# A Laplace neural operator layer and an involution block: VectorE's order in the forward transform written out by hand, its table work cut into 242 steps

## The chip, the cores and the metric

The kernel runs on one core of a Trainium2 chip. A core has five engines that run side by side, each through its own list of instructions in order: TensorE (PE, matmuls), VectorE (DVE), ScalarE (ACT), GpSimd (POOL) and SyncE (SP, which here issues DMAs; GpSimd issues some as well). They wait for one another through semaphores. Matmuls write to a small memory, PSUM; everything else lies in SBUF (128 partitions). The metric is device time in microseconds of the whole kernel, lower is better.

## What is computed

Two residual layers on x of 16 images, 16 channels, 256 x 256, float32. The first, which the change concerns, is a Laplace neural operator on the group-normalised input:

```python
alpha = jnp.fft.fft2(x, axes=(-2, -1))
A = 1.0 / (omega1[:, None, None, None] - weights_pole1[None])
Bm = 1.0 / (omega2[:, None, None, None] - weights_pole2[None])
S = jnp.einsum('ikpq,oikp,xikq->oxik', weights_residue, A, Bm)
output_residue1 = jnp.einsum('biox,oxik->bkox', alpha, S)
C = jnp.einsum('biox,oikp->bikpx', alpha, A)
D = jnp.einsum('bikpx,xikq->bikpq', C, Bm)
output_residue2 = jnp.einsum('bikpq,ikpq->bkpq', D, weights_residue)
x1 = jnp.fft.ifft2(output_residue1, s=(Ny, Nx), axes=(-2, -1)).real
E1 = jnp.exp(weights_pole1[..., None] * tyc)
E2 = jnp.exp(weights_pole2[..., None] * txc)
F = jnp.einsum('kbpq,bipz->kbiqz', output_residue2, E1)
x2 = jnp.einsum('kbiqz,biqx->kizx', F, E2).real
return x1 + x2 / Nx / Ny
```

The second layer (convolutions, mish, involution, a channel gate) is not touched.

## The kernel before

Four stages follow one another: `layer0_forward` (Fourier transform, about 0 to 1378 us of the profiled execution), `layer0_mix` (spectrum times the table of S, to about 2900), `layer0_back` (inverse transform, to about 3560) and `layer1`. The change lies in the first.

`layer0_forward` takes 64 steps, one for each image b and each group cg of four channels; two neighbouring channels make one normalisation group. A step does this:

- `fetch` (called for the input two steps ahead) loads z by SP and takes its BN statistics (L174) and aggregates (L176) on VectorE.
- `halves` (for the next step) normalises. `group_norm_scalars` sums over partitions with two small matmuls, gn_mean (L34) and gn_var (L42); VectorE works on each result (L36 to L39, then L44 and L47 to L53, with a square root on ScalarE at L46 between). Then VectorE adds the image's two halves, less the mean (L191), and GpSimd subtracts them (L194, 128 x 1024): both parts are the tile eo, which has two buffers.
- `rows`, twice for two channels each: for each channel 16 matmuls on pu (L207) and pv (L214), ScalarE copies half of pu to `right` (L222), and VectorE adds and subtracts it into u (L224, two instructions). pu has two buffers. ScalarE evicts pv as v, scaled (L231).
- `poles`: matmuls on v (L241), multiplied on VectorE (t, L252) and added up on GpSimd (acc, L265 to L267).
- `columns`: for the previous image's u, matmuls (L313), evictions on ScalarE (o, L320), stores by GpSimd (L329). Eight frequencies a step, nine in each fourth; the first four steps have none. The tile px has two buffers, which the tables' matmuls share.
- `finish`, once an image, closes the pole sums.

Beside the steps stand tables that depend on the weights alone. Two, `table("1")` and `table("2")`, are needed by `rows` and `poles` and made at the start (L135 to L140 on VectorE, matmuls L149, copies L158 and L160). Three more are needed by later stages and are written to DRAM in `tables`, a generator: residues (td, 16 channels, VectorE L415 to L426, matmuls L437), planes of A (avd, 33, L466 to L490) and exponentials (ed, 2 x 8 pairs of channels, L515 to L534, with `exponential` at L766 to L783). From step 4 on the main loop takes one piece of it in each step: 16 pieces with a residue each, 11 of three planes, 16 of a pair of exponentials, one kind after the other.

What sets the order: within `manual_schedule`, the engines named in it (here TensorE alone) run their instructions as the program is written. For the other engines a scheduler at build time orders them, and can put a table's instruction, or the statistics of an input, far from where it is written.

Of the kernel before, what the change touches and what calls it, by code (L numbers as in the profile page):

```python
# [72 lines left out]
def layer0_forward(ctx, tc, d, al, bd, tabs):  # L73
# [105 lines left out]
    def halves(b, cg, z, mv):  # L179

        if cg == 0:
            scales[b] = sm.tile([P, G], F32, tag="rs", name="rs")
        rs = scales[b][:, 2 * cg : 2 * cg + 2]
        nm = sm.tile([P, 2], F32, tag="nm", name="nm")
        yield from group_norm_scalars(nc, sm, psn, ones, mv, 2, nm, rs)
        nm2 = sm.tile([P, 2], F32, tag="nm2", name="nm2")
        nc.vector.tensor_scalar(nm2, nm, 2.0, None, ALU.mult)
        eo = ep.tile([P, 2, 4, N], F32, tag="eo", name="eo")
        for g in range(2):
            cs = slice(2 * g, 2 * g + 2)  # L190
            nc.vector.scalar_tensor_tensor(  # L191
                eo[:, 0, cs], z[:, cs, 0], nm2[:, g : g + 1], z[:, cs, 1], ALU.add, ALU.add
            )
        nc.gpsimd.tensor_tensor(eo[:, 1], z[:, :, 0], z[:, :, 1], ALU.subtract)  # L194
        yield eo, rs

    def rows(b, cg, j, eo, rs):
# [3 lines left out]
        for a in range(2):  # L201
# [21 lines left out]
            for h, sign in ((0, ALU.add), (1, ALU.subtract)):  # L223
# [5 lines left out]
                )  # L229
        vt = vp.tile([P, 2, 2, P], F32, tag="v", name="v")  # L230
# [105 lines left out]
    with tc.manual_schedule(engines={mybir.EngineType.PE}):  # L336
# [3 lines left out]
        *_, ready = halves(*steps[0], *fetched.pop(0))  # L340
        pieces = tables(ctx, tc, d, psx, tabs)
        acc = rsc = None
        for i, (b, cg) in enumerate(steps):
            now, following = ready, iter(())
            if i + 1 < len(steps):
                following = halves(*steps[i + 1], *fetched.pop(0))
                next(following)
            v0 = rows(b, cg, 0, *now)
            next(following, None)
            if b and cg == 0:  # L350
                rsc = finish(b - 1, acc)
            v1 = rows(b, cg, 1, *now)
            ready = next(following, None)
# [5 lines left out]
            poles(cg, (v0, v1), acc)  # L359
            if b:  # L360
# [4 lines left out]
            if i >= 4:  # L365
                next(pieces, None)
# [16 lines left out]
def tables(ctx, tc, d, psum, tabs):  # L383
# [5 lines left out]


    krow = load(nc, cp, d["krow_t"], [P, N], "krow_t")
    w = frequencies(nc, cp, d["tx"], krow, [P, N], "wt")
    sign = load(nc, cp, d["sign_t"], [P, 1], "sign_t")
    qr = cp.tile([P, C], F32, name="tqr")
    qi = cp.tile([P, C], F32, name="tqi")
    rr = cp.tile([P, C, M], F32, name="trr")
    ri = cp.tile([P, C, M], F32, name="tri")
    for t in range(2):
        ps = slice(64 * t, 64 * t + 64)
        nc.sync.dma_start(out=qr[ps], in_=d["p2r_iq"])  # L400
        nc.sync.dma_start(out=qi[ps], in_=d["p2i_iq"])
        nc.sync.dma_start(out=rr[ps], in_=d["rr_iq"])
        nc.sync.dma_start(out=ri[ps], in_=d["ri_iq"])
    nc.vector.tensor_scalar(qi, qi, sign, None, ALU.mult)
    nri = cp.tile([P, C, M], F32, name="tnri")
    nc.vector.tensor_scalar(nri, ri, sign, None, ALU.mult)
    nc.vector.tensor_scalar(ri, nri, -1.0, None, ALU.mult)
    q2 = cp.tile([P, C], F32, name="tq2")
    nc.vector.tensor_tensor(q2, qr, qr, ALU.mult)
    mt = load(nc, cp, d["mt"], [P, 2, 16], "mt")  # L410
    for k in range(C):
        e = tp.tile([P, N], F32, tag="te", name="te")
        r = tp.tile([P, N], F32, tag="trec", name="trec")
        br = tp.tile([P, N], F32, tag="tbr", name="tbr")
        nc.vector.tensor_scalar(e, w, qi[:, k : k + 1], None, ALU.add)  # L415
        nc.vector.tensor_tensor(r, e, e, ALU.mult)
        nc.vector.tensor_scalar(r, r, q2[:, k : k + 1], None, ALU.add)
        nc.vector.reciprocal(r, r)
        nc.vector.tensor_scalar(br, r, qr[:, k : k + 1], -1.0, ALU.mult, ALU.mult)
        nc.vector.scalar_tensor_tensor(e, e, -1.0, r, ALU.mult, ALU.mult)  # L420
        wts = []
        for h in range(2):
            wt = tp.tile([P, 2, 2, 16, M], F32, tag=f"wt{h}", name="wt")
            shape = [P, 16, M]
            for part, c, coef in ((0, 0, rr), (0, 1, ri), (1, 0, nri), (1, 1, rr)):
                nc.vector.tensor_tensor(  # L426
                    wt[:, part, c],
                    mt[:, h].unsqueeze(2).to_broadcast(shape),
                    coef[:, k].unsqueeze(1).to_broadcast(shape),
                    ALU.mult,  # L430
                )
            wts.append(wt)
        yield
        ps = psum.tile([P, 2, N], F32, tag="px", name="pt")
        for h, wt in enumerate(wts):
            for part, rhs in ((0, br), (1, e)):
                nc.tensor.matmul(  # L437
                    ps[:, h],
                    lhsT=wt[:, part].rearrange("p c i m -> p (c i m)"),
                    rhs=rhs,  # L440
                    start=part == 0,
                    stop=part == 1,
                )
        t = tp.tile([P, 2, N], F32, tag="tt", name="tt")
        nc.scalar.copy(t, ps)
        nc.sync.dma_start(out=td[:, :, k], in_=t)

    krow = load(nc, cp, d["krow_m"], [P, N], "krow_m")  # L450
    w = frequencies(nc, cp, d["ty"], krow, [P, N], "wm")
    sign = load(nc, cp, d["sign_m"], [P, 1], "sign_m")
    pr = cp.tile([P, 32], F32, name="tpr")
    pi = cp.tile([P, 32], F32, name="tpi")
    for q in range(4):
        nc.sync.dma_start(out=pr[32 * q : 32 * q + 32], in_=d["p1r_ip"])
        nc.sync.dma_start(out=pi[32 * q : 32 * q + 32], in_=d["p1i_ip"])
    nc.vector.tensor_scalar(pi, pi, sign, None, ALU.mult)
    pr2 = cp.tile([P, 32], F32, name="tpr2")
    nc.vector.tensor_tensor(pr2, pr, pr, ALU.mult)  # L460
    npr = cp.tile([P, 32], F32, name="tnpr")
    nc.vector.tensor_scalar(npr, pr, -1.0, None, ALU.mult)
    for g in range(NF):
        four = [P, 32, 4]
        e = tp.tile(four, F32, tag="ae", name="ae")
        nc.vector.tensor_tensor(  # L466
            e,
            w[:, 4 * g : 4 * g + 4].unsqueeze(1).to_broadcast(four),
            pi.unsqueeze(2).to_broadcast(four),
            ALU.add,  # L470
        )
        r = tp.tile(four, F32, tag="ar", name="ar")
        nc.vector.tensor_tensor(r, e, e, ALU.mult)
        nc.vector.tensor_tensor(r, r, pr2.unsqueeze(2).to_broadcast(four), ALU.add)
        nc.vector.reciprocal(r, r)
        av = tp.tile([P, 32, 4, 3], F32, tag="av", name="av")
        half = [64, 32, 4]
        nprb = npr.unsqueeze(2)
        nc.vector.tensor_tensor(av[:64, :, :, 1], r[:64], nprb[:64].to_broadcast(half), ALU.mult)
        nc.vector.tensor_tensor(av[64:, :, :, 1], r[64:], e[64:], ALU.mult)  # L480
        nc.vector.scalar_tensor_tensor(
            av[:64, :, :, 0].rearrange("p k f -> p (k f)"),
            e[:64].rearrange("p k f -> p (k f)"),
            -1.0,
            r[:64].rearrange("p k f -> p (k f)"),
            ALU.mult,
            ALU.mult,
        )
        nc.vector.tensor_tensor(av[64:, :, :, 0], r[64:], nprb[64:].to_broadcast(half), ALU.mult)
        nc.vector.tensor_scalar(av[:, :, :, 2], av[:, :, :, 0], -1.0, None, ALU.mult)  # L490
        nc.sync.dma_start(out=avd[g], in_=av.rearrange("p k f l -> p (k f l)"))
        if g % 3 == 2:
            yield


    phase = load(nc, cp, d["phase"], [P, 1], "phase")
    turn = cp.tile([P, 1], F32, name="turn")
    nc.vector.tensor_scalar(turn, phase, TWO_PI, None, ALU.mult)
    last = load(nc, cp, d["last"], [P, 1], "last")
    c1 = 6.28125  # L500
    c2 = float(np.float32(TWO_PI - c1))
    for i, axis in enumerate("12"):
        pr = cp.tile([P, C], F32, name=f"epr{axis}")
        pi = cp.tile([P, C], F32, name=f"epi{axis}")
        for a in range(2):
            nc.sync.dma_start(out=pr[64 * a : 64 * a + 64], in_=d[f"p{axis}r_kp"])
            nc.sync.dma_start(out=pi[64 * a : 64 * a + 64], in_=d[f"p{axis}i_kp"])
        tr = cp.tile([P, N], F32, name=f"etr{axis}")
        nc.sync.dma_start(out=tr, in_=d["ty" if axis == "1" else "tx"].to_broadcast([P, N]))
        for k in range(0, C, 2):  # L510
            arg = tp.tile([P, 2, N], F32, tag="arg", name="arg")
            n = tp.tile([P, 2, N], F32, tag="n", name="n")
            nf, af = n.rearrange("p k x -> p (k x)"), arg.rearrange("p k x -> p (k x)")
# [1024 lines left out]
```

## Time and profile before

| | |
|---|---|
| three runs | 7063.57, 7067.28, 7080.53 us (median 7067.28) |
| profiled execution | 7081.88 us in all, span 7080.1 us |
| mean TensorE clock | 0.976 of full |
| busy share: TensorE, VectorE, ScalarE, GpSimd | 92%, 79%, 54%, 50% |

The forward transform from 70 to 1380 us holds TensorE 1202.7 us busy, VectorE 1058.5, ScalarE 428.9, GpSimd 578.2.

How to read the views that follow: in the table of groups a row is a line of the kernel, an engine, an operation, the tiles written and read, its count, its busy time and its mean. In the timeline a row is start, duration, engine, line and operation; in brackets how long the engine stood idle before it and what ended that. Weight loads of TensorE have rows of their own. Times are microseconds from the start of the span, and of this one execution. Line numbers are those of the kernel before; in the changed kernel the lines below L182 are moved by two and more.

### The profile page before, as it was taken

What the parts mean: (1) busy time and instruction counts of PE and PEld (TensorE: products, weight loads), DVE (VectorE), ACT (ScalarE), POOL (GpSimd) and SP (SyncE); (2) the same over time, 40 slices, a digit from 0 to 9 for tenths busy, and PEclk for the clock granted to TensorE, in tenths of its full rate; (3) what the DMA queues carried; (4) which work ended last, traced back from release to release, by engine and by line L of the source; (5) the groups of instructions that cost most, each with busy time, mean ns of one, the idle gap of its engine ahead of it and who ended that gap; (6) DMA issues with size and microseconds to landing.
All of it is one profiled execution on the core that took longest, in us unless ns stands there. A gap on an engine that the chain in (4) does not pass through costs nothing. (4 is left out here: it accounts for less than half of the span.)

```text
span 7080.1 us, 144599 instructions
## 1 busy us (share of the span) xinstructions
PE 6544.7 (92%) x55592; PEld 3663.3 (52%) x55592; DVE 5608.9 (79%) x10346; ACT 3835.5 (54%) x5996; POOL 3521.3 (50%) x4614
## 2 busy tenths in 40 slices
PE   7889999899999998899979999999999999999996
PEld 5777778666667666677733333333333333333331
DVE  8999985466667666688878888888888888888885
ACT  2223333365666665322266666666666676666671
POOL 2334445412222222466655666667666667665663
PEclk9899999999999999999989999999999999999998
DMA  3344444433333333699968888889888889888886
GB/s 99 112 115 123 125 120 123 132 95 92 100 99 102 98 96 92 207 326 326 326 191 248 260 257 269 277 278 282 268 257 265 277 281 278 277 258 264 277 272 212
DMA packets 716083, 1443.41 MB, mean 204 GB/s; under 512 B 98954, under 2 KB 525254, under 8 KB 673638
## 3 DMA queue, kind: packets, MB, share of 16 engines
q1 hardware_dynamic: 567206, 959.76, 44.3%
q0 software_dynamic: 148192, 474.40, 21.3%
q8 instruction: 444, 7.27, 0.4%
q14 instruction: 241, 1.97, 0.1%
HBM read 877.12 MB, written 556.47 MB: 202 GB/s over the span
## 5 line engine op out<-in xcount | busy, mean ns | idle before, releaser
L1085 ACT ACTIVATE wide<-c,b 32x512 f32<-32x512 f32 x2176 | 1477.6, 679 | 314.0 <-PE c L1037 265.2
L1116 DVE TENSOR_TENSOR top<-pd,t 32x512 f32<-32x512 f32 x2176 | 1504.0, 691 | 55.8 <-DMA cf<-top 3.2
L1037 PE MATMUL c<-z,w 102*128 102x512 f32 x2048 | 996.4, 618 | 110.5 <-ACT wide L1085 89.0
L1113 DVE TENSOR_TENSOR t<-pd,r 64x512 f32<-64x512 f32 x1088 | 743.8, 684 | 349.0 <-PE pd L1105 322.8
L1097 POOL COPY wide<-wide 32x1031 f32<-32x1031 f32 (+1 forms) x576 | 581.2, 1009 | 882.6 <-ACT wide L1085 855.5
L1105 PE MATMUL pd<-wide,dw 128*128 128x512 f32 x2048 | 994.4, 607 | 13.0 <-DVE top L1116 12.0
L720 POOL DMA_DIRECT2D hd<-h x512 | 323.5, 639 | 1207.1 <-DVE h L713 1182.6
L1037 PEld LDWEIGHTS c<-z,w 102*128 102x128 f32 x2048 | 370.6, 191 | 695.2 <-issue 457.9
L1185 PE MATMUL c2ps<-rows,c 128*32 128x512 f32 x6144 | 721.9, 602 | 5.6 <-DVE odd L1212 5.6
L1105 PEld LDWEIGHTS pd<-wide,dw 128*128 128x128 f32 x2048 | 382.8, 193 | 576.5 <-issue 417.2
L1056 ACT ACTIVATE bot<-c,b 128x512 f32<-128x512 f32 x544 | 343.9, 683 | 462.2 <-issue 383.3
L1098 POOL COPY wide<-wide 32x1031 f32<-32x1031 f32 (+1 forms) x576 | 574.0, 997 | 33.5
L700 PE MATMUL ph<-ix,yt 64*128 64x256 f32 x4128 | 506.6, 393 | 6.1 <-issue 5.4
L643 PE MATMUL ps<-tt,lt 128*64 128x256 f32 x4224 | 495.4, 385 | 13.3 <-DMA tt<-td 10.4
L313 PE MATMUL px<-wxn,u 128*64 128x256 f32 x4224 | 482.9, 380 | 8.1 <-ACT o L320 8.1
L207 PE MATMUL pu<-fy,eo 128*128 128x128 f32 x2048 | 427.0, 292 | 26.4 <-DVE u L224 21.8
L700 PEld LDWEIGHTS ph<-ix,yt 64*128 64x128 f32 x4128 | 395.9, 191 | 93.7 <-issue 46.1
L1185 PEld LDWEIGHTS c2ps<-rows,c 128*32 128x32 f32 x6144 | 175.4, 109 | 513.3 <-issue 407.8
L873 POOL TENSOR_TENSOR x<-x,o 128x512 f32<-128x512 f32 x256 | 323.7, 1265 | 217.4 <-DVE o L872 199.3
L607 DVE TENSOR_SCALAR alb<-alc,m 128x1024 f32<-128x1024 f32 x330 | 420.0, 1397 | 0.0
L214 PE MATMUL pv<-at,eo 128*128 128x128 f32 x2048 | 413.9, 285 | 0.0
L651 DVE COPY s<-ps 128x512 f32<-128x512 f32 x264 | 265.4, 1023 | 186.9 <-PE ps L643 169.7
(220 smaller groups left out, 11732.0 us busy)
## 6 DMA issues: line engine op xcount, KB each, us to landing
rows<-cf SPq DMA_DIRECT2D x128, 2176.0 KB
z<-zn SPq DMA_DIRECT2D x768, 257.8 KB
cf<-top POOLq DMA_DIRECT2D x512, 240.0 KB, 6.8
cf<-bot POOLq DMA_DIRECT2D x96, 840.0 KB, 11.0
alc<-al SPq DMA_DIRECT2D x264, 256.0 KB
zn<-zb SPq DMA_DIRECT2D x128, 516.0 KB
o<-zn SPq DMA_DIRECT2D x128, 516.0 KB
z<-in_x SPq DMA_DIRECT2D x64, 1024.0 KB
```

What stands on the lines that cost most here:

```text
L207: nc.tensor.matmul(pu[:, xh, e].rearrange("p v m -> p (v m)"), lhsT=lhs, rhs=fy[:, e], start=True, stop=True,)
L313: nc.tensor.matmul(ps[64 * k : 64 * k + 64, :, h], lhsT=u[:, h, part, g0 + j + k].rearrange("p f c -> p (f c)"), rhs=wxn[:, h, part], star ...
L643: nc.tensor.matmul(ps[64 * h : 64 * h + 64, v], lhsT=lt[:, h, k, 1 - v : 3 - v].rearrange("p l f c -> p (l f c)"), rhs=tt[:, h, k], start= ...
L700: nc.tensor.matmul(ph[q][:, e], lhsT=yt[lanes, i].rearrange("p t k -> p (t k)"), rhs=ix[lanes, i], start=n == 0, stop=n == 3,)
L1037: nc.tensor.matmul(ps[:, a], lhsT=w, rhs=z[:k, c : c + 2, 0:N], start=True, stop=True)
L1085: nc.scalar.activation(self.feat[64 - 32 * q : 96 - 32 * q, f, self.groups[g], :H], ps[q][32 * f : 32 * f + 32], AF.Mish, bias=b1[0][32 * ...
L1097: nc.gpsimd.tensor_copy(flat[0:32, f, 1:m], flat[64:96, f, 0 : m - 1])
L1098: nc.gpsimd.tensor_copy(flat[96:128, f, 0 : m - 1], flat[32:64, f, 1:m])
L1105: nc.tensor.matmul(ps, lhsT=dwt if self.tail else dw, rhs=self.feat[:, f, cs, :H], start=True, stop=True,)
L1113: nc.vector.tensor_tensor(t[64:128], ps[:64], self.r[:, cs], ALU.mult)
L1116: nc.vector.tensor_tensor(self.top[32 * f : 32 * f + 32, cs, q], ps[lanes], t[lanes], ALU.add)
L1185: nc.tensor.matmul(ps[32 * j : 32 * j + 32], lhsT=w[:, blk], rhs=src[:, 4 * j + blk : 4 * j + blk + 4, x : x + H], start=(i, blk) == (0, 0 ...
```

## The change

VectorE joins TensorE in `manual_schedule`, so its instructions now run as written. What is written changes with it:

- The second half of `group_norm_scalars` (variance, root, scale) moves from between the two calls of `rows` to after `poles`; the sums and differences eo come directly after the mean.
- `tables` becomes three generators, residues, planes and exponentials, cut much finer and merged in equal proportion into 242 steps (64 places for residues, of which 49 have work, 66 for planes, 112 for exponentials). `rows` takes one behind each channel's u, from step 2 on: four a step, so that the last is taken in step 62.
- Scalings by a value per partition in the tables move from VectorE to ScalarE.

```diff
@@ halves
-        yield from group_norm_scalars(nc, sm, psn, ones, mv, 2, nm, rs)
+        scalars = group_norm_scalars(nc, sm, psn, ones, mv, 2, nm, rs)
+        next(scalars)
...
         yield eo, rs
+        yield from scalars
@@ rows
-    def rows(b, cg, j, eo, rs):
+    def rows(b, cg, j, eo, rs, between):
...
+            next(between, None)
         vt = vp.tile([P, 2, 2, P], F32, tag="v", name="v")
@@ main loop
-    with tc.manual_schedule(engines={mybir.EngineType.PE}):
+    with tc.manual_schedule(engines={mybir.EngineType.PE, mybir.EngineType.DVE}):
...
             if i + 1 < len(steps):
                 following = halves(*steps[i + 1], *fetched.pop(0))
-                next(following)
-            v0 = rows(b, cg, 0, *now)
-            next(following, None)
+                ready = next(following)
+            v0 = rows(b, cg, 0, *now, pieces if i >= 2 else iter(()))
             if b and cg == 0:
                 rsc = finish(b - 1, acc)
-            v1 = rows(b, cg, 1, *now)
-            ready = next(following, None)
+            v1 = rows(b, cg, 1, *now, pieces if i >= 2 else iter(()))
...
             poles(cg, (v0, v1), acc)
+            next(following, None)
             if b:
                 for g0 in range(8 * cg, 8 * cg + 8 if cg < 3 else NF, 4):
                     columns(b - 1, g0, rsc)
             if i + 2 < len(steps):
                 fetched.append(fetch(*steps[i + 2]))
-            if i >= 4:
-                next(pieces, None)
@@ tables, residues (one channel k)
-        nc.vector.tensor_scalar(e, w, qi[:, k : k + 1], None, ALU.add)
-        nc.vector.tensor_tensor(r, e, e, ALU.mult)
-        nc.vector.tensor_scalar(r, r, q2[:, k : k + 1], None, ALU.add)
-        nc.vector.reciprocal(r, r)
-        nc.vector.tensor_scalar(br, r, qr[:, k : k + 1], -1.0, ALU.mult, ALU.mult)
+            nc.scalar.activation(e, w, AF.Identity, bias=qi[:, k : k + 1])
+            nc.vector.tensor_tensor(r, e, e, ALU.mult)
+            nc.scalar.activation(r, r, AF.Identity, bias=q2[:, k : k + 1])
+            nc.vector.reciprocal(r, r)
+            yield
+            nc.scalar.activation(br, r, AF.Copy, scale=nqr[:, k : k + 1])
...
                 wts.append(wt)
+                yield
@@ tables, planes (one g)
             nc.vector.reciprocal(r, r)
+            yield
...
-        nc.vector.tensor_scalar(av[:, :, :, 2], av[:, :, :, 0], -1.0, None, ALU.mult)
+            nc.scalar.activation(av[:, :, :, 2], av[:, :, :, 0], AF.Copy, scale=-1.0)
             nc.sync.dma_start(out=avd[g], in_=av.rearrange("p k f l -> p (k f l)"))
-        if g % 3 == 2:
-            yield
+            yield
@@ tables, exponentials (a pair of channels)
                 for j in range(2):
-                nc.vector.tensor_scalar(arg[:, j], tr, pi[:, k + j : k + j + 1], None, ALU.mult)
+                    nc.scalar.activation(arg[:, j], tr, AF.Copy, scale=pi[:, k + j : k + j + 1])
...
                 nc.vector.scalar_tensor_tensor(af, nf, -c1, af, ALU.mult, ALU.add)
+                yield
...
                 nc.scalar.activation(n, arg, AF.Sin)
                 for j in range(2):
-                nc.vector.tensor_scalar(arg[:, j], tr, pr[:, k + j : k + j + 1], None, ALU.mult)
-            exponential(nc, tp, af)
+                    nc.scalar.activation(arg[:, j], tr, AF.Copy, scale=pr[:, k + j : k + j + 1])
+                yield
+                yield from exponential_steps(nc, tp, af)
                 if axis == "2":
-                nc.vector.tensor_scalar(n, n, last, None, ALU.mult)
+                    nc.scalar.activation(n, n, AF.Copy, scale=last)
@@ tables, the end
+    parts = ((residues(), 4 * C), (planes(), 2 * NF), (exponentials(), 7 * C))
+    order = sorted(((i + 0.5) / n, p) for p, (_, n) in enumerate(parts) for i in range(n))
+    for _, p in order:
+        next(parts[p][0], None)
+        yield
+    for part, _ in parts:
+        for _ in part:
+            pass
@@ exponential, now a generator of four steps
+def exponential_steps(nc, pool, y):
...
     nc.vector.scalar_tensor_tensor(y, n, -c1, y, ALU.mult, ALU.add)
+    yield
     nc.vector.scalar_tensor_tensor(y, n, -c2, y, ALU.mult, ALU.add)
...
     nc.vector.tensor_scalar(n, y, 1 / 5040, None, ALU.mult)
-    for c in (1 / 720, 1 / 120, 1 / 24, 1 / 6, 1 / 2, 1.0):
+    yield
+    for i, c in enumerate((1 / 720, 1 / 120, 1 / 24, 1 / 6, 1 / 2, 1.0)):
         nc.vector.scalar_tensor_tensor(n, n, c, y, ALU.add, ALU.mult)
+        if i % 3 == 2:
+            yield
```

## The prediction

> **What bounds the kernel now.** Only the forward transform changes, so I read the busy time in 40 us windows first, for where it is short of TensorE's limit. Columns: window, length, then busy us (and instructions) of TensorE, its weight loads, VectorE, ScalarE, GpSimd, then TensorE clock, DMA share, GB/s.
>
> ```profile
> 180.00:220.00 40.00, 33.05 (x272) 28.89 (x272) 35.27 (x108) 10.36 (x20) 11.03 (x13) 0.87 0.38 112
> ...
> 420.00:460.00 40.00, 35.29 (x309) 28.51 (x308) 36.70 (x109) 12.49 (x21) 16.08 (x23) 0.91 0.41 117
> ...
> 780.00:820.00 40.00, 35.22 (x344) 28.51 (x338) 37.14 (x97) 14.94 (x28) 18.50 (x26) 1.00 0.42 113
> ...
> 1140.00:1180.00 40.00, 40.00 (x406) 34.19 (x406) 23.43 (x74) 13.40 (x28) 18.60 (x25) 1.00 0.49 137
> ```
>
> While tables are made (to 1040 us) VectorE is full and TensorE has holes; afterwards TensorE is full and VectorE has 40% to spare. That slack is what spreading the tables is after. The waits of TensorE in this stage (total us, times, longest) say what holds it:
>
> ```profile
> PE gn_var L42 <- DVE gnq L39: 63.7, 22, 5.3
> PE pu L207 <- DVE u L224: 21.8, 21, 1.9
> ```
>
> The timeline then gives the step: L241, once a step, is its clock. A step without tables:
>
> ```profile
> 1300.07 2.04 PE L241 MATMUL pd<-bt,v 128*64 128x128 f32 x32
> ...
> 1308.95 0.38 PE L34 MATMUL gn_mean<-mv,ones 128*128 128x2 f32 x2
> ...
> 1309.37 0.16 DVE L36 TENSOR_TENSOR gnq<-mv,gn_mean 128x2 f32<-128x2 f32 x1 [6.39 <-PE gn_mean L34]
> ...
> 1309.83 1.41 DVE L191 SCALAR_TENSOR_TENSOR eo<-z,nm 128x512 f32<-128x512 f32 x2
> ...
> 1311.48 1.03 DVE L224 TENSOR_TENSOR u<-pu,right 128x256 f32<-128x256 f32 x2 [0.23 <-ACT right L222]
> ...
> 1316.73 2.04 PE L241 MATMUL pd<-bt,v 128*64 128x128 f32 x32
> ```
>
> 16.66 us, all TensorE; one in four takes 19.09 (fifth column group, `finish`): 17.3 on average. Read the same way, L241 starts at 112.42 in step 1 and at 1332.95 in step 63: 1220.5 us, 19.7 a step. Steps 5 to 20 take about 25, steps 21 to 47 about 19. At most 62 x (19.7 - 17.3) = 149 us can be won, some 29 less for the tables' own matmuls (16 times 1.84 us, L437).
>
> One more row matters. The second VectorE line is two elements wide and takes 0.17 us otherwise:
>
> ```profile
> 944.54 2.75 POOL L194 TENSOR_TENSOR eo<-z 128x1024 f32<-128x1024 f32 x1 [4.48 <-PE pv L214]
> ...
> 944.98 2.34 DVE L52 TENSOR_SCALAR gnt<-gnt 128x2 f32<-128x2 f32 x1
> ...
> 1314.76 0.17 DVE L52 TENSOR_SCALAR gnt<-gnt 128x2 f32<-128x2 f32 x1
> ```
>
> It ended when GpSimd's subtraction ended. L52, L53, L297, L473, L479, L490 and L519 all have cases of 1.3 to 2.9 us there; L224 and L252 (PSUM inputs) and L174 have none.
>
> **The Trainium skill.** "SBUF — State Buffer", Who interferes with whom: a VectorE instruction with two SBUF inputs, or in a two-port mode, and a GpSimd instruction that reads SBUF exclude each other; the later one waits for the whole of the earlier. The trace agrees, as above. "TensorE: Matmul & The Clock Gate", What's actually happening: the clock halves after an idle window and returns after a busy one. Here holes of 2.4 us and more (L42 after 3.83 us) were followed by 2 to 5 us of L207 at 0.42 us a pair instead of 0.22; of some 20 holes up to 1.92 us one was. "ScalarE: Activation LUTs", What ACT_TABLE_LOAD costs: about 1.28 us; the rows here have 1283 ns, and sin and square root still alternate 16 times.
>
> **The change, part by part.** (a) Scalings to ScalarE: L415, L417, L419, L490, L515, L525, L528 were 5.4+5.5+5.9+11.7+10.4+10.1+3.8 = 53 us of VectorE. ScalarE, 54% busy over the span and about a third here, has room; but in the first third of a residue step VectorE now waits for ScalarE and back. Bounds 0.1 and 1.3 us a time; I take 0.6.
>
> (b) Order. In the built program's order VectorE's step is a closed ring: BN statistics and aggregate of the input two steps ahead come last, and TensorE's first instruction of the next step, L34, waits for that aggregate with all of the next rows behind it. Before, the scheduler put the statistics earlier: L36 waited 6.39 us for TensorE, not TensorE for it. The ring's fixed part, from the timeline: aggregate to L36 through L34 0.5; L36 to nm2 0.46; eo 1.41; until the first u 0.23; four pairs of u, 0.88 start to start, 3.5; t 0.75; L44, root on ScalarE, back 0.5; L47 to L53 1.0; statistics 2.4; aggregates 0.33; `finish` 0.9 each fourth step. Sum 11.3, less 0.3 where a u begins before a table step has drained: 11.0.
>
> (c) The table steps are now chains of dependent operations; each pays its whole row plus 0.04. Before, other work was laid between and such operations overlapped by 0.07 to 0.1. From the rows by shape (L782 0.68, L418 1.74, L475 0.94, the rest likewise, with the lock cases taken out): a pair of exponential channels 1.7+1.7+2.1+2.0+2.2+2.2+1.8 = 13.6, 16 times, 218; a plane 1.95+1.4 = 3.35, 33 times, 110; a residue 2.8+1.0+0.6 = 4.4, 16 times, 70. That is 398 us, 6.4 a step over 62 steps (the residues end at the 49th of their 64 places).
>
> (d) The lock. GpSimd's subtraction starts when TensorE ends a step's rows. The fourth channel's matmuls wait for the second channel's u (two pu buffers), end 1.9 us after it, and the subtraction ends 4.3 after it. VectorE then has a table step (1.6) and the third pair of u (1.0) and meets the lock with its next table step at about 2.6: 1.7 us. Bounds 0 (it falls on u, t or statistics) and 2.4. The acc additions (0.72+0.45+0.45) catch L50 to L53: 0.3.
>
> Ring: 11.0 + 6.4 + 1.7 + 0.3 = 19.4. TensorE's own step, with the wait at the fourth channel, is 17.4, plus 1.84 with a residue's matmuls and 0.7 to 0.9 in two of four. I took the longer of both step by step: 1218 us for 62 steps. Added: 16 sins, each delaying the root behind a table reload by 0.8 on average, 13; half clock where the hole before L34 passes 2.4 us (four or five heavy steps), 8; less 10 for the empty places late, where the lock finds nothing. 1229 against 1220.5: +9.
>
> (e) Start. The second table's first half was interleaved ahead of the first rows; now all its VectorE work (four times 6.5 us, the 3.3 us reciprocal in it) comes after the first u, and its second half only after L160 has read the first half's matmuls (64 of L149 at 0.44, 28 us, half of them exposed). L241 of step 0 moves from 102.7 to about 121, the first rows starting some 6 us sooner included; step 1, now a ring without tables (14 us for 9.7), loses 4 more: +22. Bounds 10 and 30.
>
> (f) At no cost: z is issued about two steps ahead, behind table stores on SP's queue that wait for ScalarE; td, avd and ed are complete, but for one plane and one pair, a step before the mix begins. If that cover goes, a few us once. The setup loads (about 30 on SP) end before VectorE reaches them.
>
> Sum: +9 + 22 = +31 on the profiled execution's 7080.1 us of span (7081.9 in all), 7113. That execution is 14.6 above the median 7067.3; on the median's level I say **7098**.
>
> **Rivals.** Faster: the lock mostly misses. Without it the ring is 17.7 and TensorE (18.3 on average) decides; the longer of both is about 18.6, 62 times 1153 + 13 - 1220.5 + 22 = -32: 7035; with the start hidden too, 7013. For it: VectorE's slack after 1040 us is real, and 53 us leave it. Against it: GpSimd's start hangs on VectorE's own u, so the meeting recurs each step. It decides where the stall is under 0.9 us a step.
>
> Much slower: the hole before L34 exceeds 2.4 us in most steps, the first two channels run at half clock, each ring grows by about 1.6, and ScalarE's fixed order (root or a table result ahead of a copy) adds some: 21.5 a step, 1333, +135: 7200. For it: every long hole had this. Against: my holes are 1 to 2 us.
>
> A wash: a stall of 1.2 us (-31) and a start of +15 (-7) leave -7, within measurement.
>
> **How the numbers follow.** Forecast (own range 7070 to 7140) 0.60, faster rival 0.18, much slower 0.10, wash 0.12. What a measurement of this kernel can tell from no change is 0.3%, 21 us; about a sixth of the forecast's chance lies below 7088 and counts as the same. Slower 0.50 + 0.10 = 0.60, same 0.10 + 0.12 = 0.22, faster 0.18. The range takes the faster rival in at its likely value and stops short of the slowest: 7030 to 7170.
>
> **What would show it.** L241 steps of 19 to 21 us in all of steps 3 to 62, none at 16.66 before the last; L34 waiting for the aggregate (L176), a TensorE wait that isn't there now; table operations of 1.5 to 2.5 us beside GpSimd's eo nearly every step; L241 of step 0 near 121 us; clock about 1.0 after 200 us. Wrong if steps of 17 to 18 us fill the stage (lock missed), or if L207 at 0.42 us a pair recurs each step.

## The result, and the profile after

The changed kernel takes 7171.03 us (median of four runs, 7161.94 to 7183.55) against 7073.9 us (median of four) for the kernel before: ratio 1.0137, 95% interval 1.0125 to 1.0149. The profiled execution's span is 7172.5 us against 7080.1, 92.4 more, at a mean TensorE clock of 0.974 against 0.976. The forecast was slower by 31 us, 7098 in all: the direction was right, the size a third of what came, and 7171 lies just above the range that ended at 7170. Of the 73 us between 7098 and 7171, 6.6 come from the level: the kernel before stood that much above its earlier median of 7067.3. The other 66 are the change's.

Line numbers are now the changed kernel's. L34 to L53 are as before; L174, L176 stay; eo is L192 on VectorE and L195 on GpSimd; the rows' matmuls are L209 and L216, `right` L224, u L226, v L234, the pole matmuls L244, t L255, column matmuls L316, their evictions L323.

The same windows as before, same columns (TensorE, its loads, VectorE, ScalarE, GpSimd, clock, DMA share, GB/s):

```profile
180.00:220.00 40.00, 29.94 (x260) 26.68 (x260) 34.15 (x89) 7.01 (x17) 7.93 (x8) 0.81 0.20 60
420.00:460.00 40.00, 36.93 (x348) 29.45 (x345) 36.01 (x94) 16.37 (x30) 18.35 (x27) 1.00 0.42 115
...
780.00:820.00 40.00, 34.99 (x320) 27.92 (x321) 32.73 (x91) 11.45 (x24) 17.36 (x25) 0.96 0.36 105
1140.00:1180.00 40.00, 38.24 (x369) 30.73 (x366) 36.93 (x92) 13.50 (x26) 18.91 (x26) 1.00 0.43 118
```

The tables are spread: VectorE's work at 1140 us rose from 23.43 to 36.93 us and TensorE's fell there from 40.00. At 420 us TensorE is a little busier than before (36.93 for 35.29). But at 780 us, where it was to be relieved too, it is not (34.99 for 35.22), and VectorE is less busy (32.73 for 37.14): both wait. What each waits for between 166 and 1412 us (total us, times, longest):

```profile
PE gn_mean L34 <- DVE mv L176: 77.1, 38, 12.7
PE px L316 <- ACT o L323: 22.0, 22, 3.4
PE pu L209 <- DVE u L226: 14.1, 24, 1.3
PE pd L244 <- ACT v L234: 10.8, 8, 4.4
```

```profile
DVE gnq L36 <- PE gn_mean L34: 53.8, 60, 3.6
DVE gnr L47 <- ACT gnr L46: 36.7, 60, 4.8
DVE u L226 <- ACT right L224: 19.6, 18, 2.1
```

L34 waits for L176, the closed ring of part (b) of the prediction, a wait that the kernel before didn't have. And VectorE waits at L36 for the answer in nearly every step. One step of the timeline has it all:

```profile
608.05 0.33 DVE L176 BATCH_NORM_AGGREGATE mv<-st 128x2 f32<-128x12 f32 x2
608.43 0.59 PE L34 MATMUL gn_mean<-mv,ones 128*128 128x2 f32 x2 [2.75 <-DVE mv L176]
...
610.72 0.64 PE L209 MATMUL pu<-fy,eo 128*128 128x128 f32 x2
611.15 0.63 PE L216 MATMUL pv<-at,eo 128*128 128x128 f32 x2
...
612.71 1.03 DVE L226 TENSOR_TENSOR u<-pu,right 128x256 f32<-128x256 f32 x2 [1.58 <-ACT right L224]
...
615.45 0.39 PE L209 MATMUL pu<-fy,eo 128*128 128x128 f32 x2
...
619.27 2.36 POOL L195 TENSOR_TENSOR eo<-z 128x1024 f32<-128x1024 f32 x1 [9.06 <-PE pv L216]
619.70 2.11 DVE L485 TENSOR_TENSOR av<-ar,tnpr 64x128 f32<-64x128 f32 x1
...
628.18 2.46 DVE L174 BATCH_NORM_STATS2 st<-z 128x6 f32<-128x512 f32 x4
630.56 0.33 DVE L176 BATCH_NORM_AGGREGATE mv<-st 128x2 f32<-128x12 f32 x2
631.13 0.38 PE L34 MATMUL gn_mean<-mv,ones 128*128 128x2 f32 x2
```

Read it from the top. TensorE stood 2.75 us before L34, and its next matmuls run at half clock (two in 0.43 us start to start; from 615.45 on two in 0.22), so VectorE stands 1.58 us before the first u. Then L485, 0.32 us otherwise, takes 2.11: it ends 0.18 us after GpSimd's subtraction does. The step ends with the statistics, and L34 follows 0.24 us after the aggregate's end.

The start, TensorE's rows and two of VectorE's:

```profile
80.10 3.78 PE L149 MATMUL aps<-q,wx 128*128 128x512 f32 x4 [10.03 <-DVE q L140]
86.78 15.24 PE L149 MATMUL aps<-q,wx 128*128 128x512 f32 x28 [2.91 <-DVE q L140]
...
110.27 3.43 PE L149 MATMUL aps<-q,wx 128*128 128x512 f32 x4 [8.25 <-DVE q L140]
116.87 13.86 PE L149 MATMUL aps<-q,wx 128*128 128x512 f32 x28 [3.17 <-DVE q L140]
130.66 1.97 PE L244 MATMUL pd<-bt,v 128*64 128x128 f32 x32
```

```profile
102.68 0.69 DVE L160 TENSOR_SCALAR bt<-aps 128x512 f32<-128x512 f32 x1 [6.17 <-ACT bt L158]
105.32 3.35 DVE L138 RECIPROCAL q<-q 128x512 f32<-128x512 f32 x1
```

VectorE waits at L160 until the first half's matmuls are done, and only then begins the second half's quotients; TensorE waits for those. Neither engine's work covers the other's.

Where the 92 us came from, by the first L244 of a step (before in brackets): step 0 at 130.7 (102.7), step 1 at 148.2 (112.4), step 2 at 165.6 (125.0), step 62 at 1411.4 (1316.7), step 63 at 1428.1 (1333.0). So 35.7 us of it were there at step 1, 59.4 more came in the 62 steps after, and all that follows took 2.8 less. The 59.4 are a balance. Read the same way, steps 5 to 20, where the tables lay thickest before, became 60 us shorter (341 for 402), so the spreading did pay there. Steps 2 to 4 became 29 us longer, steps 21 to 47 became 58 us longer (566 for 508), and steps 48 to 62 became 33 us longer (292 for 260).

### The profile page after: what moved, and what is told of

Same layout as the page of the kernel before. It is cut to its first block, busy times and chain, and to the rows that moved or that the text cites. A ratio compares the mean times of both kernels' runs of the same rounds, so it can differ in the third digit from the quotient of the medians.

```text
span 7172.5 us, 144629 instructions
## 1 busy us (share of the span) xinstructions
PE 6572.7 (92%) x55592; PEld 3659.2 (51%) x55592; DVE 5681.8 (79%) x10194; ACT 3894.7 (54%) x6149; POOL 3508.8 (49%) x4614
## 5 line engine op out<-in xcount | busy, mean ns | idle before, releaser
L316 PE MATMUL px<-wxn,u 128*64 128x256 f32 x4224 | 495.2, 384 | 22.7 <-ACT o L323 22.3
L209 PE MATMUL pu<-fy,eo 128*128 128x128 f32 x2048 | 419.4, 288 | 18.3 <-DVE u L226 14.1
L216 PE MATMUL pv<-at,eo 128*128 128x128 f32 x2048 | 408.6, 282 | 0.0
```

What stands on the lines that cost most here:

```text
L316: nc.tensor.matmul(ps[64 * k : 64 * k + 64, :, h], lhsT=u[:, h, part, g0 + j + k].rearrange("p f c -> p (f c)"), rhs=wxn[:, h, part], star ...
```

## The experiments

All but e15, which starts from the kernel before, are the changed kernel with the edit shown, and all compute the whole result. Edits are shortened. The first four undo or move one part each.

```diff
 e1
     v0 = rows(b, cg, 0, *now, pieces if i >= 2 else iter(()))
+    fetched.append(fetch(*steps[i + 2]))     # was the last call of the step
     rsc = finish(b - 1, acc)                 # first step of an image only
     v1 = rows(b, cg, 1, *now, pieces if i >= 2 else iter(()))
 e2
-    nc.gpsimd.tensor_tensor(eo[:, 1], z[:, :, 0], z[:, :, 1], ALU.subtract)
+    nc.vector.tensor_tensor(eo[:, 1], z[:, :, 0], z[:, :, 1], ALU.subtract)
 e3  (seven scalings of this kind)
-    nc.scalar.activation(e, w, AF.Identity, bias=qi[:, k : k + 1])
+    nc.vector.tensor_scalar(e, w, qi[:, k : k + 1], None, ALU.add)
 e4
-    nc.vector.tensor_scalar(dst[:, :, planes[2]], src, -1.0, None, ALU.mult)
+    nc.scalar.activation(dst[:, :, planes[2]], src, AF.Copy, scale=-1.0)
```

> One part changed: the BN statistics of the input two steps ahead (L174, L176) stand in VectorE's order between the two pairs of rows, no longer at the end of the step; everything else as in the changed kernel. A, the closed ring (TensorE's first instruction L34 waits for the aggregate at the end of VectorE's step, then VectorE for TensorE): of VectorE's 20.7 us a step 10.8 are fixed work, 6.2 tables, 1.8 lock, 2.3 waits; with the ring open the step is VectorE's own 19 to 19.5, L34's wait for L176 is gone, steps 2 to 62 take 1150 to 1175 us for 1246 and the whole 7070 to 7100. B, ScalarE's order (copies and square roots behind table scalings) makes the extra: it stays, steps 2 to 62 take over 1225 and the whole 7150 or more.

> One part changed: the odd half of eo is subtracted on VectorE instead of GpSimd, after the even half. A, the lock costs what it shows (1.7 us a step of stretched table operations): it goes, about 1.35 us of subtraction comes, steps 2 to 62 some 20 to 25 us shorter than 1246, the whole 7140 to 7155. B, the stretched operations only fill time in which VectorE would wait for TensorE or ScalarE anyway: the subtraction's 1.35 us a step comes on top, steps 2 to 62 take 1290 to 1325 and the whole 7220 to 7255.

> One part undone: the tables' scalings (L418, L420, L423, L496, L521, L532, L536) are back on VectorE, in the same places of the same order; sine, square root and the copies stay on ScalarE. A, VectorE's own length sets the step: 53 us of work come back, about 30 us of waits for ScalarE (L418 and L420 19, L521 5, L532 6) go: steps 2 to 62 take 1260 to 1275 for 1246, the whole 7185 to 7200. B, ScalarE's order sets the extra (copies of right and v and the square roots queued behind scalings that wait for VectorE): their waits of 0.3 us and 0.3 us a step and TensorE's holes go too, steps 2 to 62 take 1200 to 1235 and the whole 7120 to 7160.

> One part changed: the negated plane of the second table (L160, four instructions) is written by ScalarE, not VectorE. A, in VectorE's order L160 keeps the second half's quotients (13.5 us) behind the first half's matmuls, so neither covers the other: freed of it they overlap, the first L244 comes at 115 to 119 us for 130.7, and the whole gains 11 to 16 us, 7155 to 7160. B, the start is limited by TensorE's half clock and the quotients themselves: first L244 at 128 or later and no change of the whole over 4 us.

Measured, as median, ratio to the kernel before with its 95% interval, first L244 of step 0, and the time from step 2's L244 to step 62's (of one profiled execution each). The kernel before has its median in the runs beside e1 to e4:

| | us | ratio | L244, step 0 | steps 2 to 62 |
|---|---|---|---|---|
| before | 7074.3 | 1 | 102.7 | 1191.7 |
| changed | 7171.0 | 1.0137 (1.0125 to 1.0149) | 130.7 | 1245.8 |
| e1 ring open | 7105.0 | 1.0044 (1.0030 to 1.0059) | 130.7 | 1198.6 |
| e2 subtraction on VectorE | 7134.9 | 1.0087 (1.0072 to 1.0102) | 128.8 | 1218.2 |
| e3 scalings on VectorE | 7204.8 | 1.0183 (1.0168 to 1.0198) | 130.3 | 1282.3 |
| e4 L160 on ScalarE | 7153.5 | 1.0111 (1.0096 to 1.0127) | 116.3 | 1245.3 |

e4 is the cleanest: the start gets 14.4 us shorter and the steps after it don't change. TensorE's two halves are now one stretch:

```profile
87.35 29.06 PE L149 MATMUL aps<-q,wx 128*128 128x512 f32 x60 [2.90 <-DVE q L140]
116.34 1.97 PE L244 MATMUL pd<-bt,v 128*64 128x128 f32 x32
```

e2: 27.6 us fewer in the steps although VectorE has 1.22 us more to do in each: the stretched operations are real time on the path. GpSimd, freed of the subtraction, also issues the column stores; but ScalarE's waits for those stores are much the same (25.0 us for 29.5), so the gain doesn't lie there. e3: 34 us slower in all, the direction of theory A and a little more than its 7185 to 7200; in this order the scalings were worth moving. e1: L34's wait for L176 is gone from the trace, and 66 us with it; but the steps take 1198.6, more than the 1150 to 1175 of A. Two things are left over. In the first step of an image `finish` now stood behind the statistics, and TensorE waited for it, 34.1 us in all:

```profile
PE pd L244 <- DVE u L297: 23.0, 8, 6.8
...
PE pd L244 <- DVE r L289: 11.1, 7, 2.3
```

And VectorE's wait at L36 grew, from 0.90 to 1.47 us a step.

The next four try ScalarE's order, which A of e1 had left out, the scheduler, and sums.

```diff
 e5, e8
-    with tc.manual_schedule(engines={PE, DVE}):
+    with tc.manual_schedule(engines={PE, DVE, Activation}):
...
     nc.scalar.copy(right, pu[:, 1])
+    if a:
+        nc.scalar.activation(vt, pv, AF.Copy, scale=rs[:, j : j + 1])
+    for _ in held:                # the table step of the channel before
+        next(between, None)
...
 e6
-    with tc.manual_schedule(engines={PE, DVE}):
+    with tc.manual_schedule(engines={PE}):
 e7, e8 (with e2 and e4)
     rsc = finish(b - 1, acc)
+    next(following, None)         # L42 to L53, were behind the poles
+    fetched.append(fetch(*steps[i + 2]))
     v1 = rows(b, cg, 1, *now, pieces if i >= 2 else iter(()))
```

> One part changed: ScalarE's order is written out too. In it the copy of the next channel (and v) stands ahead of a table step's scalings, and the square root ahead of the column copies; VectorE keeps its order but for finish, one table step earlier in it. A, what the closed ring adds beyond its own work is ScalarE's order (the scheduler put the first column copy, which waits for TensorE, ahead of the square root, and scalings that wait for VectorE ahead of right and v): L47's wait for L46 falls to 0.3 us, L226's wait for right goes, steps 2 to 62 take 1185 to 1215 us for 1246, the whole 7110 to 7140. B, VectorE's work and lock set the step whatever ScalarE's order: steps 2 to 62 stay over 1235, the whole 7155 or more.

> One part undone: VectorE's order is left to the scheduler again; the 242 small steps, their places in the program and the scalings on ScalarE stay. A, the written order is the loss: the scheduler puts the statistics and the second table's quotients ahead as before, L34's wait for L176 is gone, the first L244 comes before 110 us, and the whole takes 7030 to 7090. B, the small steps and the round trips to ScalarE are the loss: the whole stays at 7130 or more.

> Three parts together: the ring opened at both ends (the statistics and aggregate of two steps ahead, and L42 to L53, stand between the two pairs of rows, behind finish), the odd half of eo on VectorE, L160 on ScalarE. A, the three losses are separate: single gains of about 66, 36 and 18 us add up, and finish no longer behind the statistics gives 10 to 20 more: 7030 to 7055. B, they hide each other, and both engines in fixed orders meet at about 19.5 us a step whatever is taken off VectorE: 7070 to 7090.

> As the run before with ScalarE's order written out too, copies and square root ahead of the table scalings. A, ScalarE's order costs beside the ring: 20 to 40 us less than the run before, 7000 to 7030. B, with the ring open ScalarE's delays are absorbed: within 8 us of the run before.

e5: 7230.7 us, 1.0224 (1.0207 to 1.0241), slower than the changed kernel; e8: 7201.9, 1.0186 (1.0170 to 1.0201), 91 us slower than e7, which neither theory had. The theory that this order of ScalarE would take the extra away falls. L47's wait for the root stayed where it was (34.8 us for 36.7 in the window above). What the scheduler had done was better than it looked: with the root written ahead of the column copies, ScalarE stands at the root until VectorE comes to L44, and TensorE waits for the copies behind it. TensorE's and ScalarE's waits in e5, where L316 and L323 are L320 and L327:

```profile
PE px L320 <- ACT o L327: 109.6, 51, 5.5
```

```profile
ACT gnr L46 <- DVE gnv L44: 191.3, 49, 7.2
```

e6: 7052.6 us, 0.9978 (0.9969 to 0.9986): one word less in the list of engines takes 118 us off and beats the kernel before. The first L244 comes at 103.2, steps 2 to 62 take 1168.9. So of the change it is VectorE's written order that loses; the rest of it, left to a free order, gains a little. L34's wait for L176 is gone; what is left of TensorE's waits is mainly

```profile
PE pu L209 <- DVE u L226: 41.7, 30, 3.1
```

e7: 7110.5, 1.0056 (1.0041 to 1.0071), no faster than e1 alone, though it holds e1's, e2's and e4's edits. The gains do not add up, and even B's 7070 to 7090 was too low. With L42 to L53 in the middle VectorE waits there for ScalarE's root (1.05 us a step for 0.60 in the changed kernel), and TensorE for u behind them, 65.5 us for 14.1:

```profile
PE pu L209 <- DVE u L226: 65.5, 52, 4.1
```

That the new place of L42 to L53 is the cause is not shown: e13 below is this kernel with them back behind the poles, and it is only 14 us faster, with intervals that overlap.

Then sizes within a free order, and the ring opened better.

```diff
 e9   e6 with e3's edit          e10  e6 with e4's edit          e11  e6 with e2's edit
 e12  e4 with
     rsc = finish(b - 1, acc)
+    fetched.append(fetch(*steps[i + 2]))     # was the last call of the step
     v1 = rows(b, cg, 1, *now, pieces if i >= 2 else iter(()))
```

> VectorE's order left to the scheduler, and the tables' scalings back on VectorE: of the change only the spreading in small steps is left. A, taking 53 us off VectorE is what made the version with a free order (7052.6) faster than before: without it the time is before's or a little more, 7065 to 7095. B, the spreading made it: the scalings matter little, 7045 to 7060.

> VectorE's order left to the scheduler, L160 on ScalarE. A, in a free order L160 is already out of the quotients' way: the first L244 stays at 101 to 104 us, the whole within 6 us of 7052.6. B, it still delays the second table: first L244 before 97 us, the whole 7040 to 7046.

> VectorE's order left to the scheduler, the odd half of eo subtracted on VectorE. A, the lock costs in a free order what it costs in a written one, since GpSimd's subtraction meets VectorE's table operations either way: 15 to 35 us less than 7052.6, 7018 to 7038. B, in a free order the stretched operations fall into time in which VectorE would wait for TensorE: no gain or a loss, 7048 to 7085.

> VectorE's order written out. The statistics of two steps ahead stand between the two pairs of rows as in the first run here, but behind finish, and L160 is on ScalarE. A, opening the ring at the statistics is worth its 66 us, and what the first run lost (34 us of TensorE waiting for finish's L289 and L297) comes back: 7060 to 7080, as fast as before. B, the waits only change place (L36 for TensorE, L47 for ScalarE): 7085 to 7105.

| | us | ratio | L244, step 0 | steps 2 to 62 |
|---|---|---|---|---|
| e6 free order | 7052.6 | 0.9978 (0.9969 to 0.9986) | 103.2 | 1168.9 |
| e9 and scalings on VectorE | 7047.2 | 0.9966 (0.9958 to 0.9975) | 103.9 | 1163.2 |
| e10 and L160 on ScalarE | 7059.4 | 0.9983 (0.9977 to 0.9990) | 103.2 | 1172.9 |
| e11 and subtraction on VectorE | 7020.8 | 0.9926 (0.9907 to 0.9945) | 106.4 | 1140.2 |
| e12 written, ring open behind finish | 7071.9 | 1.0002 (0.9993 to 1.0010) | 115.3 | 1176.8 |

e10 gives nothing, as A had it: L160 costs only where it is written ahead of the quotients. e11: without the lock 32 us go, though VectorE gets the subtraction. e9 is against my part (a): in a free order the scalings on ScalarE bring nothing. e12 confirms A: its steps 2 to 62 take 1176.8 us for the changed kernel's 1245.8, and it is as fast as the kernel before.

But why? I added up, over steps 5 to 62, what VectorE instructions beside GpSimd's arithmetic took beyond the lower quartile of their own form: 1.90 us a step in the changed kernel, 0.88 in e1, 0.79 in e12. Beside the subtraction alone it is 1.66, 0.50 and 0.40. In e2 and e13, where GpSimd subtracts nothing, 0.21 and 0.42 are left. The ring's opening took most of the lock away. The timeline of e12 shows how:

```profile
711.36 2.46 DVE L174 BATCH_NORM_STATS2 st<-z 128x6 f32<-128x512 f32 x4
711.72 2.36 POOL L195 TENSOR_TENSOR eo<-z 128x1024 f32<-128x1024 f32 x1 [3.99 <-PE pv L216]
```

The statistics now stand where GpSimd subtracts, and run on beside it at their usual pace, four in 2.46 us. Over all steps from 200 us, 1.32 us of statistics and 0.51 of u lie beside one subtraction in e12; in the changed kernel 0.42 of u and none of the statistics. That left open whether the ring has a cost of its own:

```diff
 e13  e12 with e2's edit
 e14  e11 with e3's edit
 e15  the kernel before with e2's edit
```

> VectorE's order written out, statistics behind finish and L160 on ScalarE as in the run before it (7071.9), and the odd half of eo subtracted on VectorE too. A, ring and lock are separate costs: the subtraction gains again what it gained alone, 25 to 40 us: 7030 to 7047. B, the ring costs by bringing the lock about (VectorE comes back from its wait at the time at which GpSimd subtracts): with the ring open only 0.8 us a step of lock is left, less than the subtraction's 1.35 us: 7070 to 7110.

> VectorE's order free, the subtraction on VectorE (7020.8), and the tables' scalings back on VectorE: of the change only the small steps are left. A, the scalings on ScalarE bring nothing beside it (VectorE waits for ScalarE's results as long as it is relieved), as in the free order before: 7010 to 7025. B, with the subtraction VectorE is fuller and the 53 us count: 7030 to 7060.

> The kernel before with one line changed: the odd half of eo subtracted on VectorE. A, the small steps of the change are worth what the version with a free order shows (about 20 us), and the subtraction the rest: 7025 to 7045. B, the whole gain is the subtraction's: 7000 to 7012. C, with the coarse steps the subtraction brings nothing: 7060 or more.

e13: 7096.5, 1.0039 (1.0025 to 1.0053), 25 us slower than e12: B. While GpSimd subtracts, opening the ring shortens steps 2 to 62 by 68.5 us (1245.3 in e4, 1176.8 in e12). Once VectorE subtracts, it shortens them by 16.1 (1218.2 in e2, 1202.1 in e13; e2 leaves L160 on VectorE, which e4 showed to matter at the start alone). So about three quarters of what the ring seemed to cost was the lock that it brought about. The size of the lock agrees: 1.1 us a step less of it, 1.1 us a step gained. That a VectorE with the subtraction to do would gain as much from an open ring as one without it is taken for granted here, and wasn't tested. TensorE waits for u nearly as long in e13 as in e7:

```profile
PE pu L209 <- DVE u L226: 49.8, 51, 3.4
```

e14: 7004.8 us, 0.9904 (0.9889 to 0.9919), the lowest of all. That is 16 us below e11, but the two intervals overlap: that the scalings do better on VectorE once the lock is gone isn't shown. What e9 and e14 do show is that in a free order they gain nothing by being on ScalarE. Why isn't settled; both theories of e14 expected 7010 or more.

e15: 7028.0, 0.9941 (0.9925 to 0.9958). So the subtraction's one line is worth 43 us to the kernel before, and the change's small steps in a free order 23 more (e14). The 43 us are more than a sum of VectorE's work gives: counted as above, the lock beside the subtraction was 1.07 us a step there, and the subtraction itself takes 1.22. What got shorter is TensorE's waits for VectorE, 63.7 and 21.8 us before:

```profile
PE gn_var L42 <- DVE gnq L39: 44.4, 15, 4.0
PE pu L207 <- DVE u L224: 13.6, 20, 2.2
```

ScalarE's waits for GpSimd's stores fell by 6 us only, to 19.7. So the lock seems to cost by where it falls, too; which operations carry that is open.

## Why the prediction was wrong in size

**(a) Scalings.** Right for this order: taking them back costs 34 us (e3). This part priced the work leaving VectorE and not the order it sits in; in the free order it was worth nothing (e9, e14).

**(b) The ring.** The mechanism is there, and the term that failed is its waits. The sum had about 1.6 us of waiting a step: 0.5 at L36, 0.2 for the first u, 0.3 for the root, 0.15 for the residues' round trips, and 26 us over the steps for TensorE's longer ones, sines, half clock and empty places (1218 less 62 times 19.4, and 13, 8 and -10). Measured over steps 5 to 62, the step is 20.71 us. VectorE waits 2.42 of it: at L36 0.90, at L47 0.60, for `right` 0.31, for the residues' ScalarE results 0.33, for the other table scalings and sines 0.21, for a table's store 0.06. The rest, 18.28, is its work with the gaps below 0.12 us between instructions; the sum, which counts such gaps in part (c), had 18.2. So the work was right, and the 0.8 us a step, 50 us in all, that are missing are the waits.

So the step that failed is the sum's pricing of the waits, 1.6 us where 2.4 came: it took the longer of two engines step by step, which lets a delay cost only once, on the engine that is longer. In the runs the delay is handed on: L34 waits for VectorE (77.1 us), VectorE's L36 then waits for L34's answer in 60 of 60 steps (53.8 us), and L47 for the root (36.7). And waits removed at one point come back in part at another: in e1 L34's wait for L176 went, and L36's rose to 1.47 us a step. That this handing on is what the sum lacked is argued from these waits; no experiment sets it apart.

**(c) Table steps.** 6.4 us a step predicted, 6.2 measured (forms' lower quartiles, without the lock and the short gaps). A pair's seven figures sum to 13.7 and not 13.6, which is nothing here.

**(d) The lock.** 2.0 predicted with the acc additions, 1.9 measured, over half a microsecond in 50 of 58 steps. Wrong was to treat it as one term beside the ring: it went when the ring was opened, and made about three quarters of what the ring cost. Nor did the forecast set against it that the kernel before had 1.2 of it already. As for the Trainium skill, "SBUF — State Buffer", Who interferes with whom, also says that a VectorE instruction with at most one SBUF input, outside the two-port modes, is not excluded. L174 at its full speed beside L195 agrees (2.46 us for four, above), and the sentence would have told where to put it.

**(e) Start.** +22 predicted at step 1, +35.7 measured. At step 0 it is 28.0 against some 18. The mechanism named is there, VectorE held at L160; what it costs was read wrongly. The 64 matmuls of L149, 28 us, are those of both halves, 32 each, and they stood bare in front of the first pole matmuls before, too:

```profile
73.97 10.46 PE L149 MATMUL aps<-q,wx 128*128 128x512 f32 x24
85.27 17.53 PE L149 MATMUL aps<-q,wx 128*128 128x512 f32 x40 [0.83 <-DVE bt L160]
```

New are TensorE's waits for the second table's quotients, 24.4 us in the rows of the changed kernel above (10.03, 2.91, 8.25 and 3.17). Behind them the matmuls start at half clock, 0.85 us apart for 0.43, so that the 64 take 36.3 us for 28.0. These 8.3 us, which the sum had nowhere, are most of what it lacked at step 0. L160's place makes 14.4 of the 28.0 (e4). Steps 1 and 2 then took 17.5 us each for 9.7 and 12.6: TensorE stood 4.6 and 4.9 us before L34 and ran the first rows at half clock. With the ring open they take 11.6 and 12.1 (e1).

**Half clock.** "Four or five heavy steps" were nine, of eleven with a hole of 2.4 us or more before L34; each has 15 to 28 matmuls at about 0.1 us more. But the kernel before had half clock as well, behind its holes before L42: in steps 2 to 62 its clock stood at half for 81.9 us, the changed kernel's for 75.1. So in these steps half clock is no part of what the change added. TensorE's time in these steps without its waits did rise by 15 us (1093.7 to 1108.7), in the column matmuls (L316, 14 us more) and the pole matmuls (L244, 11 more), while the rows' fell; why is open. And of the 18 holes of 1.0 to 1.92 us of the kernel before, two were followed by half clock (730.8 and 973.2 us), where the prediction has one.

**(f)** Nothing came after the forward transform: 2.8 us less. But the first table steps hold about 4 us of setup arithmetic on VectorE that the sum left out, and step 2 takes 25.2 us.

**The signs named beforehand.** Right: L34 waiting for L176, table operations of about 2 us beside GpSimd nearly each step, none at 16.66 before the last. Wrong: L244 of step 0 at 130.7 instead of 121; steps of 17.3 to 27.9 us where 19 to 21 were named; a clock of 0.90 to 1.0 after 260 us where about 1.0 was expected from 200. The faster rival is out: the lock did not miss. The much slower one was right that long holes before L34 bring half clock, in fewer steps than it supposed; for its other part, ScalarE's order, there are 22.0 us of TensorE's waits for L323, but the one other order that was tried (e5) was slower.

## What to carry to other kernels

Before writing an engine's order out, ask whether the last thing in its step is what the next step's first instruction needs, and put that thing early; and count a wait for each point at which two fixed orders meet, not just the longer of two sums. Where two engines lock each other out of SBUF, look in the trace for an instruction that keeps its usual time there (here the statistics, u, whose other input is in PSUM, and reciprocals, L421 with 1.75 us beside it and elsewhere) and place it there. One SBUF input alone is not enough: scalings with one were held, L528 up to 2.65 us for 0.49. Or move the work to the engine that was blocked. A scheduler's odd-looking order is worth a run with one engine freed before it is overruled: that run gained 118 us here.

## What was unexpected of the hardware

- A VectorE operation of 1.22 us a step (the subtraction) was cheaper than the same on GpSimd at 2.4 us beside it: 36 us in the written order, 32 in the free one, 43 in the kernel before.
- Four statistics of 128 x 512 took 2.46 us beside GpSimd's subtraction as elsewhere, while two-input operations of 64 x 128 (0.32 us) and of eight elements (L300, 2.30 for 0.13 in two cases) were held up to its end.
- Of eleven holes of 2.4 us or more before L34, nine were followed by half clock, two (3.2 and 2.8 us) were not; of those of 2.0 and 2.3 none.
